# A state-space block ahead of experts and local attention: the scan's drive, the gate, softplus, the convolution's taps, TensorE's start and two small rank tensors rearranged

## The chip, the cores and the metric

The kernel runs on one core of one Trainium2 chip. A core has five engines with queues of their own, each of which runs its instructions in the order in which they were written: TensorE (PE, the matrix array, with weight loads shown as PEld), VectorE (DVE), ScalarE (ACT), GpSimd (POOL) and SyncE (SP, which here only issues DMAs). SBUF is the on-chip memory, PSUM the small one that TensorE writes to. The metric is the device time of one execution in microseconds (us), the median of several; less is better.

## What is computed

A decoder of one block: a state-space layer with a mixture of eight experts behind it, a cross-attention with a relative bias, and six layers of local attention and feed-forward. There are two batches of 512 tokens, 128 features. The change lies in the state-space layer and in the routing of tokens to experts:

```python
def mamba_block(x, in_proj_w, conv_w, conv_b, x_proj_w, dt_proj_w, dt_proj_b, A_log, D_skip, out_proj_w):
    xz = x @ in_proj_w                          # x: (2, 512, 128), xz: (2, 512, 512)
    xi, z = jnp.split(xz, 2, axis=-1)           # 256 channels each
    xc = conv(xi, conv_w)                       # causal, per channel, 4 taps
    xi = jax.nn.silu(xc + conv_b)
    dbc = xi @ x_proj_w                         # 64 + 16 + 16 columns
    delta = jax.nn.softplus(dbc[..., :64] @ dt_proj_w + dt_proj_b)
    Bm, Cm = dbc[..., 64:80], dbc[..., 80:]     # 16 states
    A = -jnp.exp(A_log)
    # for each time step t, channel e and state n:
    #   h = exp(delta * A) * h + (delta * xi) * Bm ;  y = sum over n of h * Cm
    y = y + D_skip * xi
    y = y * jax.nn.silu(z)                      # the gate
    return y @ out_proj_w

def moe_block(x, router_w, Wg, Wu, Wd):         # rms-normed x
    rw = jax.nn.softmax(hs @ router_w)          # 8 experts
    top_w, sel = jax.lax.top_k(rw, 2)
    # out = sum over the two chosen experts of
    #   top_w * ((silu(hs @ Wg[e]) * (hs @ Wu[e])) @ Wd[e])
```

Around both are rms norms and residual additions. The cross-attention and the six layers follow; the change doesn't touch them.

## The kernel before

The program is written out in full, with no loops on the chip. The engines' queues have the order of the text (`manual_schedule`); Python generators are stepped in turn to interleave several streams, so that the place of a `yield` decides what stands behind what in a queue. Waits between engines are put in by the framework where an instruction reads or overwrites what another wrote. Buffers of one tag are handed out in turn, and a new one waits until the oldest has been read for the last time.

**Start.** `norm_in` (L217) norms the tokens of a batch: a square on ScalarE, a sum on VectorE, then six small GpSimd steps for the inverse root (`rstd`, L165), and a product on VectorE. For the first batch GpSimd also multiplies the four taps of the convolution into the input projection (`wk`, L223), so that convolution and projection are one set of matmuls. `turn_in` (L228) transposes the tokens on TensorE against the identity matrix `ident`, sets three columns of zeros ahead of them on GpSimd (L230) and copies them to `nT` on ScalarE (L231). `conv` (L233) has four matmuls for each half of the 256 channels, `gate` (L239) one, `dt_b_c` (L244) two, whose 96 rows are copied to `dbc`; 32 of them, B and C of the 16 states, go to DRAM (`bcd`, L252). A float32 matmul shows as two instructions. PSUM banks come from `bank`: tag m has three, x one, da and y two each.

**Softplus.** `delta` (L254) has a matmul to a PSUM bank `pv` and then, per half of the channels, five ScalarE steps (Relu to `dl`, Abs, twice Exp, Ln) and three VectorE steps (L268 to L270) that join them with a correction for small values. Then `dx` = `dl` * `xi` (L847 for the first batch on VectorE, L876 for the second on GpSimd).

**The scan.** `scan` (L273) goes through the 16 states, each with both halves of the channels over all 512 time steps. Per state n:
- `fetch(n)`: a DMA spreads B's row over all partitions (`b_sb`, three buffers); where GpSimd does the product with C, a second DMA spreads C's row (`c_sb`, two buffers). SP issues them for the first batch, ScalarE's queue for the second.
- `drive(n)`: GpSimd multiplies `dx` with `b_sb` to `db` (three buffers; L300, for state 0 in two halves, L303).
- `decay(n, half)`: ScalarE's Exp to a PSUM bank `da` (L292, two banks).
- The scan proper: a VectorE instruction per half (L325, L328) from `da` and `db` to `hs` (three buffers).
- The product with C in place, on GpSimd (L331) for states 2, 5, 8, 11, 14 of the first batch and all even ones of the second, otherwise on VectorE (L333), with C's row spread by TensorE (`spread_c`, L309).
- `gather(n)`: TensorE adds `hs` to the sum over the states `y` (L313).

The generator yields twice per state, after each half. Ahead of the loop stand `fetch(0)`, `fetch(1)`, `drive(0)` and both `decay` of state 0; in round n come `fetch(n + 2)`, `spread_c(n)` and `drive(n + 1)`, then the scan of the first half of n.

**What runs beside it.** Beside the first batch's scan `other_batch` (L849) brings the second batch up to its own scan: its convolution, then on ScalarE a change of the activation table (L855), the silus of `xi` and of the gate, a change back, then dbc, softplus and `dx`. Beside the second batch's scan run `route(0)`, `sort(0)`, which find the two experts of each token, and the first experts of batch 0 (`experts`, L511: gathers of 128 rows each, issued by GpSimd, L529; transposes, matmuls to `gu_ps`, L546, and `xd`, L567; VectorE's L557 and L558). Tables for the cross-attention (`cross_tables`) are made there too; one of them, `crep`, takes a buffer of the tag hs for a while. `sort` (L378) counts on VectorE how many experts of a token score higher (`rank`, L402), picks ranks 0 and 1 (`sel`, L405), adds up places with matmuls, and gets each token's place `at` (L438), from which L442 on derive tables of rows; most of its tiles are small and lie in SBUF, some in the used PSUM banks. `experts(0)`'s tile `xd` is the one bank of tag x.

Of the kernel before, what the change touches and what calls it, by code (L numbers as in the profile page):

```python
# [15 lines left out]
AF = mybir.ActivationFunctionType  # L16
ALU = mybir.AluOpType
# [4 lines left out]
B, S, D = 2, 512, 128  # L22
NT = B * S
P = 128

DI, NS, KC, DTR, NE, FF = 256, 16, 4, 64, 8, 512
# [15 lines left out]
C_DTB = C_CONVB + 2  # L42
# [24 lines left out]
def decoder_kernel(ctx: ExitStack, tc: tile.TileContext, t: dict, out: bass.AP):  # L67
    nc = tc.nc
    mm, tr = nc.tensor.matmul, nc.tensor.transpose
# [9 lines left out]
    ident = const.tile([P, P], F32, name="ident")  # L79
# [5 lines left out]
    one_c = const.tile([P, 1], F32, name="one_c")  # L85
# [25 lines left out]
    NTB = S // P  # L111

    def bank(name, tag="m"):
        return ps.tile([P, S], F32, tag=tag, name=name, bufs={"m": 3, "x": 1, "da": 2, "y": 2}[tag])
# [17 lines left out]
    w_in = load(sp, [P, 2 * DI], "w_in", t["L0_attn_in_proj_w"])  # L132
    cw = sp.tile([P, KC, DI], F32, tag="hs", name="cw", bufs=3)
# [17 lines left out]
    def col(i, n=P):  # L151
        return cols[0:n, i : i + 1]
# [55 lines left out]
    wk = sp.tile([P, KC, DI], F32, name="wk")  # L208
    nTs = [sp.tile([P, KC - 1 + S], F32, name=f"nT{b}") for b in range(B)]
# [3 lines left out]
    for b in range(B):  # L213
        for name, kept in (("sz", sz), ("xi", xi), ("dl", dl), ("dx", dx)):
            kept.append(full(f"{name}{b}", "A", 8))

    def norm_in(b):  # L217
        xb = xtok[:, 4 * b : 4 * b + 4]
        ss = sq_sum(xb, f"rms1_{b}")
        r = rstd(ss, f"rms1_{b}")  # L220
        if b == 0:

            nc.gpsimd.tensor_mul(wk, cw, w_in[:, 0:DI].unsqueeze(1).to_broadcast([P, KC, DI]))  # L223
        xn = tok(f"xn{b}")
        times(xn, xb, r)
        return xn

    def turn_in(b, xn):  # L228
        pt = turn(xn, f"nT_ps{b}")
        nc.gpsimd.memset(nTs[b][:, 0 : KC - 1], 0.0)  # L230
        nc.scalar.activation(nTs[b][:, KC - 1 :], pt, AF.Identity, scale=col(C_RMS1))  # L231

    def conv(b, hf):  # L233
# [5 lines left out]
    def gate(b, hf):  # L239
        pm = bank(f"gate{b}{hf}")  # L240
        mm(pm, w_in[:, DI + hf * P : DI + (hf + 1) * P], nTs[b][:, KC - 1 :], start=True, stop=True)
        return pm
# [11 lines left out]
    def delta(b, hf):  # L254


        pv = bank(f"dl_ps{b}{hf}")
        mm(pv, w_dt[:, hf * P : (hf + 1) * P], dbcs[b][0:DTR], start=True, stop=True)
        ea, la = (sp.tile([P, S], F32, tag=n, name=n, bufs=2) for n in ("ea", "la"))
        dv = dl[b][:, hf]  # L260
        nc.scalar.activation(dv, pv, AF.Relu, bias=col(C_DTB + hf))

        nc.scalar.activation(pv, pv, AF.Abs, bias=col(C_DTB + hf))
        nc.scalar.activation(ea, pv, AF.Exp, scale=-1.0)
        nc.scalar.activation(pv, pv, AF.Exp, scale=-1.0)
        nc.scalar.activation(la, ea, AF.Ln, bias=one_c)
        yield
        nc.vector.scalar_tensor_tensor(pv, ea, 2.0, pv, ALU.subtract, ALU.mult)  # L268
        nc.vector.scalar_tensor_tensor(pv, pv, -0.5, la, ALU.mult, ALU.max)
        nc.vector.tensor_add(dv, dv, pv)  # L270
        yield

    def scan(b, on_pool):  # L273

        py = [bank(f"y{b}{hf}", "y") for hf in range(2)]
        das, dbs, bbs, cbs, pcs, hss = {}, {}, {}, {}, {}, {}
        queue = nc.scalar if b else nc.sync

        def fetch(n):
            if n < NS:  # L280
                bbs[n] = half(f"b_sb{b}_{n}", "bb", 3)
                queue.dma_start(out=bbs[n], in_=bcds[b][n : n + 1, :].to_broadcast([P, S]))
                if n in on_pool:
                    cbs[n] = half(f"c_sb{b}_{n}", "cb", 2)
                    queue.dma_start(
                        out=cbs[n], in_=bcds[b][NS + n : NS + n + 1, :].to_broadcast([P, S])
                    )

        def decay(n, hf):
            if n < NS:  # L290
                da = das[n, hf] = bank(f"da{b}_{n}{hf}", "da")
                nc.scalar.activation(  # L292
                    da, dl[b][:, hf], AF.Exp, scale=acol[:, hf * NS + n : hf * NS + n + 1]
                )

        def drive(n):
            if n < NS:
                db = dbs[n] = full(f"db{b}_{n}", "db", 3)
                if n:
                    nc.gpsimd.tensor_mul(db, dx[b], bbs[n].unsqueeze(1).to_broadcast([P, 2, S]))  # L300
                else:
                    for hf in range(2):
                        nc.gpsimd.tensor_mul(db[:, hf], dx[b][:, hf], bbs[n])  # L303

        def spread_c(n):
            if n < NS and n not in on_pool:
                pc = pcs[n] = bank(f"c_ps{b}_{n}")
                row = ident[DTR : DTR + 2 * NS, DTR + NS + n : DTR + NS + n + 1]
                mm(pc, row.to_broadcast([2 * NS, P]), dbcs[b][DTR:], start=True, stop=True)  # L309

        def gather(n):
            for hf in range(2):
                mm(py[hf], ident, hss[n][:, hf], start=n == 0, stop=n == NS - 1)  # L313

        fetch(0)
        fetch(1)
        drive(0)
        decay(0, 0)
        decay(0, 1)
        for n in range(NS):  # L320
            fetch(n + 2)
            spread_c(n)
            drive(n + 1)
            hs = hss[n] = full(f"hs{b}_{n}", "hs", 3)
            nc.vector.tensor_tensor_scan(hs[:, 0], das[n, 0], dbs[n][:, 0], 0.0, ALU.mult, ALU.add)  # L325
            decay(n + 1, 0)
            yield
            nc.vector.tensor_tensor_scan(hs[:, 1], das[n, 1], dbs[n][:, 1], 0.0, ALU.mult, ALU.add)  # L328
            decay(n + 1, 1)
            if n in on_pool:  # L330
                nc.gpsimd.tensor_mul(hs, hs, cbs[n].unsqueeze(1).to_broadcast([P, 2, S]))  # L331
            else:
                nc.vector.tensor_mul(hs, hs, pcs[n].unsqueeze(1).to_broadcast([P, 2, S]))  # L333
            if n:
                gather(n - 1)
            yield
        gather(NS - 1)
        for hf in range(2):
            yg = xi[b][:, hf]
            nc.vector.scalar_tensor_tensor(py[hf], yg, col(C_DSKIP + hf), py[hf], ALU.mult, ALU.add)  # L340
            nc.vector.tensor_mul(yg, py[hf], sz[b][:, hf])
# [33 lines left out]
    def small(name, shape, dtype=F32, bufs=1):  # L375
        return ep.tile([P, *shape], dtype, tag=name, name=name, bufs=bufs)

    def sort(b):  # L378
# [19 lines left out]
        nc.vector.tensor_mul(eqv, eqv, lt)  # L398
        nc.vector.tensor_tensor(gt, other, own, ALU.is_gt)
        nc.vector.tensor_add(gt, gt, eq)  # L400
        rank = small("rank", [NTB, NE])
        nc.vector.tensor_reduce(rank, gt, AX.X, ALU.add)  # L402
        sel, two = small("sel", [2, NTB, NE], bufs=2), small("two", [NTB, NE], BF16)
        for j in range(2):
# [28 lines left out]
        nc.vector.tensor_add(  # L433
            place, pos.rearrange("p (n e) -> p n e", e=NE), first.unsqueeze(1).to_broadcast([P, NTB, NE])
        )
        mine, at = small("mine", [2, NTB, NE]), small("at", [2 * NTB])
        nc.vector.tensor_mul(mine, sel, place.unsqueeze(1).to_broadcast([P, 2, NTB, NE]))
        nc.vector.tensor_reduce(at.rearrange("p (j n) -> p j n", j=2), mine, AX.X, ALU.add)  # L438
        yield
# [387 lines left out]
    with tc.manual_schedule(engines={ET.PE, ET.Activation, ET.DVE, ET.Pool, ET.SP}):  # L827
        xn = norm_in(0)
        nc.scalar.activation(acol, cols[:, C_ALOG : C_ALOG + 2 * NS], AF.Exp)
        nc.gpsimd.tensor_scalar(acol, acol, -1.0, None, ALU.mult)  # L830
        turn_in(0, xn)
        xn = norm_in(1)
        p0, p1 = conv(0, 0), conv(0, 1)
        for hf, pm in enumerate((p0, p1)):
            nc.scalar.activation(xi[0][:, hf], pm, AF.Silu, bias=col(C_CONVB + hf))
        p0, p1 = gate(0, 0), gate(0, 1)
        for hf, pm in enumerate((p0, p1)):
            nc.scalar.activation(sz[0][:, hf], pm, AF.Silu)
        table("natural_log_exp_and_others")
        dt_b_c(0)  # L840
        turn_in(1, xn)
# [7 lines left out]
        def other_batch():  # L849

            p0, p1 = conv(1, 0), conv(1, 1)
            yield
            yield
            table("silu_and_others")
            for hf, pm in enumerate((p0, p1)):  # L855
                nc.scalar.activation(xi[1][:, hf], pm, AF.Silu, bias=col(C_CONVB + hf))
            p0, p1 = gate(1, 0), gate(1, 1)
            for hf, pm in enumerate((p0, p1)):
                nc.scalar.activation(sz[1][:, hf], pm, AF.Silu)
            table("natural_log_exp_and_others")  # L860
            yield
            yield
            dt_b_c(1)
            yield
            nc.scalar.copy(hot, stage[:, K_HOT : K_HOT + P])
            nc.scalar.copy(masks, stage[:, K_MASK : K_MASK + 2 * S].rearrange("p (a s) -> p a s", a=2))
            nc.scalar.copy(tri, cst[:, K_TRI - K_HM1 : K_TRI - K_HM1 + P])
            yield
            for hf in range(2):
                g = delta(1, hf)  # L870
                step(g)
                yield
                yield
                step(g)
                yield
            nc.gpsimd.tensor_mul(dx[1], dl[1], xi[1])  # L876
# [34 lines left out]
    NTB = S // P  # L911
# [820 lines left out]
```

## Time and profile before

| what | us |
|---|---|
| runs | 1276.31, 1278.65, 1279.38 |
| median | 1278.65 |
| the profiled execution | 1274.54 |
| its span, first to last instruction | 1272.8 |
| start to the first scan instruction (L325) | 33.2 |
| first batch's scan, to the first sum of y with D (L340) | 33.2 to 99.4 |
| second batch's scan, to the same place | 99.4 to 202.2 |
| second batch's routing and the experts, cross-attention | to 318 |
| six layers | 318 to 1272.8 |

Busy time in three stretches, in us:

| stretch | TensorE | VectorE | ScalarE | GpSimd |
|---|---|---|---|---|
| 0 to 33.2 | 20.0 | 8.9 | 16.1 | 9.2 |
| 33.2 to 99.4 | 56.7 | 53.9 | 35.5 | 51.0 |
| 99.4 to 205.0 | 80.2 | 80.6 | 34.6 | 71.5 |

The page's views: busy time of each engine; the span in 40 slices with a digit for the busy tenths and the granted TensorE clock; DMA queues; the chain that ended last, followed back from the last instruction; the costliest groups of instructions. A line of the timeline has start and duration in us, engine, line of the program, operation, output<-inputs, shape, count, and in brackets how long the engine had been idle and what ended that.

### The profile page before, as it was taken

How to read it: one execution, taken by the hardware profiler on the slowest of the kernel's cores; microseconds unless marked ns; L12 is line 12 of the kernel's file. 1: busy time of each engine (PE TensorE's matmuls, PEld its weight loads, DVE VectorE, ACT ScalarE, POOL GpSimd, SP SyncE). 2: the span in 40 equal slices, each digit the busy share in tenths (PEclk: the TensorE clock that was granted, in tenths of full speed). 3: DMA queues.
4: the chain of work that ended last, by engine and by line, in shares of the span. 5: the costliest groups of instructions: out<-in, count | busy, mean ns of one | idle time of the engine just before them, and what ended most of it. 6: DMA issues, size and time to landing. Idle time of an engine off the chain costs nothing.

```text
span 1272.8 us, 38004 instructions
## 1 busy us (share of the span) xinstructions
PE 1121.3 (88%) x16629; PEld 729.5 (57%) x16629; DVE 868.3 (68%) x1196; ACT 641.4 (50%) x1132; POOL 692.6 (54%) x704
## 2 busy tenths in 40 slices
PE   5987688778568999999999999999999999899987
PEld 2323367766336656666666665656666666555666
DVE  2788585566776776767677766767677666676654
ACT  4643243233334565655557565655556455564543
POOL 2687662453534756646565655647555564555541
PEclk9987799799889999999999999999999999999998
DMA  4224655685102102111211102111211110110100
GB/s 117 77 67 106 195 168 146 203 286 153 53 11 82 40 19 81 53 44 38 71 53 43 45 20 81 53 31 40 81 36 39 45 36 14 36 31 20 36 15 18
DMA packets 51889, 88.52 MB, mean 70 GB/s; under 512 B 7086, under 2 KB 23852, under 8 KB 51724
## 3 DMA queue, kind: packets, MB, share of 16 engines
q1 hardware_dynamic: 46796, 76.78, 19.7%
q10 hardware_dynamic: 3456, 6.29, 1.9%
q0 software_dynamic: 1472, 3.02, 1.1%
q8 instruction: 131, 2.15, 0.7%
q14 instruction: 34, 0.28, 0.1%
HBM read 58.92 MB, written 3.19 MB: 49 GB/s over the span
## 4 chain that ended last, share of the span: by engine, by line
PE 63%; ACT 9%; DVE 7%; issue 4%; POOL 4%; DMA 0%; SPq 0%; POOLq 0%; DVEq 0%; ACTq 0%
PE qk_ps L979 11%; PE t_ps L1161 8%; PE wo_ps L1151 7%; PE v_ps L1012 7%; PE av L1100 5%; PE sim L1064 4%; PE gu_ps L546 3%; ACT pT L1162 3%; PE fo_ps L1253 2%; PE t_ps L1130 2%; PE fg_ps L1230 2%; PE sim L1053 2%; ACT oT L1132 2%; PE xd L567 2%; POOL t L1026 1%
## 5 line engine op out<-in xcount | busy, mean ns | idle before, releaser
L1000 POOL TENSOR_TENSOR t<-t,t 128x1024 f32<-128x1024 f32 x94 | 222.6, 2370 | 157.4 <-DVE t L995 156.6
L979 PE MATMUL qk_ps<-wqkv,z 128*128 128x512 f32 x384 | 186.6, 610 | 1.3 <-ACT sq L984 0.8
L1026 POOL TENSOR_TENSOR t<-t,rn 128x1024 f32<-128x1024 f32 x94 | 177.2, 1906 | 3.7
L991 DVE TENSOR_TENSOR t<-qk_ps,tab 128x1024 f32<-128x1024 f32 x96 | 117.5, 1224 | 78.5 <-PE qk_ps L979 78.5
L1161 PE MATMUL t_ps<-ident,t 128*128 128x128 f32 x768 | 104.1, 279 | 26.0 <-ACT pT L1162 10.8
L1161 PEld LDWEIGHTS t_ps<-ident,t 128*128 128x128 f32 x768 | 87.9, 144 | 64.1 <-issue 36.5
L1023 POOL TENSOR_SCALAR ss<-ss 128x32 f32<-128x32 f32 x47 | 13.4, 286 | 198.3 <-ACT sc L1022 198.3
L1004 DVE TENSOR_REDUCE ss<-sq 128x16 f32<-128x1024 f32 x96 | 116.3, 1212 | 4.0 <-ACT sq L984 0.2
L1162 ACT COPY qT<-t_ps 128x512 f32<-128x512 f32 x96 | 51.9, 588 | 128.4 <-PE t_ps L1161 128.3
L995 DVE TENSOR_TENSOR t<-qk_ps,tab 128x1024 f32<-128x1024 f32 x96 | 116.5, 1214 | 0.0
L1075 DVE TENSOR_REDUCE m<-sim 128x16 f32<-128x1024 f32 x48 | 58.8, 1224 | 70.6 <-PE sim L1064 70.6
L984 ACT ACTIVATE sq<-qk_ps 128x1024 f32<-128x1024 f32 x96 | 97.6, 1036 | 12.9 <-DVE t L995 12.9
L979 PEld LDWEIGHTS qk_ps<-wqkv,z 128*128 128x128 f32 x384 | 69.5, 197 | 52.9 <-issue 49.5
L1012 PE MATMUL v_ps<-wqkv,z 128*128 128x512 f32 x192 | 96.0, 622 | 0.5 <-issue 0.5
L1151 PE MATMUL wo_ps<-oT,wo 128*128 128x256 f32 (+1 forms) x400 | 90.3, 381 | 3.3 <-ACT oT L1132 3.3
L1100 PE MATMUL av<-vb,pT 64*32 64x65 f32 x3072 | 83.0, 228 | 8.1 <-issue 5.2
L1100 PE MATMUL av<-va,pT 64*32 64x65 f32 x3072 | 84.0, 228 | 4.2 <-issue 4.2
L1151 PEld LDWEIGHTS wo_ps<-oT,wo 128*128 128x128 f32 x400 | 74.2, 196 | 19.7 <-ACT oT L1132 6.5
L1162 ACT COPY pT<-t_ps 128x512 f32<-128x512 f32 x96 | 51.6, 589 | 62.1 <-PE t_ps L1161 62.1
L1014 ACT COPY va<-v_ps 128x1024 f32<-128x1024 f32 x48 | 48.6, 1013 | 65.1 <-PE v_ps L1012 65.1
L1064 PEld LDWEIGHTS sim<-kT,qT 64*32 64x32 f32 x6144 | 64.8, 107 | 28.4 <-issue 26.7
L313 PE MATMUL y<-hs,ident 128*128 128x512 f32 x128 | 71.2, 690 | 10.8 <-POOL hs L331 7.3
(351 smaller groups left out, 2298.2 us busy)
## 6 DMA issues: line engine op xcount, KB each, us to landing
w<-in_experts_dram SPq DMA_DIRECT2D x90, 256.0 KB, 4.7
vb<-va SPq DMA_DIRECT2D x48, 390.0 KB, 4.0
wqkv<-in_L_ffn_Wqkv_dram SPq DMA_DIRECT2D x18, 512.0 KB, 7.8
vb<-va SPq DMA_DIRECT2D x36, 130.0 KB, 3.6
b_sb<-bcd SPq DMA_DIRECT2D x16, 256.0 KB, 3.6
b_sb<-bcd ACTq DMA_DIRECT2D x16, 256.0 KB, 3.4
wo<-in_L_ffn_Wo_dram SPq DMA_DIRECT2D x6, 512.0 KB, 4.6
c_sb<-bcd ACTq DMA_DIRECT2D x8, 256.0 KB
```

What stands on the lines that cost most here:

```text
L979: mm(pa[:, hf * S : (hf + 1) * S], self.xb, w[:, w0 : w0 + S], start=True, stop=True)
L991: nc.vector.tensor_mul(t1, pa.rearrange("p (h d) -> p h d", d=DH), tab[:, 2 * qk, ti, :].unsqueeze(1).to_broadcast([P, H, DH]),)
L995: nc.vector.tensor_mul(t2.rearrange("p h (x d) -> p h x d", x=2), swap_halves(pa), tab[:, 2 * qk + 1, ti, :].rearrange("p (x d) -> p x d", ...
L1000: self.calc.tensor_add(t1, t1, t2)
L1004: nc.vector.tensor_reduce(self.ss[:, qk], self.sq[qk], AX.X, ALU.add)
L1012: mm(pv[:, hf * S : (hf + 1) * S], self.xb, w[:, w0 : w0 + S], start=True, stop=True)
L1026: self.calc.tensor_mul(self.rot[qk], self.rot[qk], self.rn[:, qk].unsqueeze(2).to_broadcast([P, H, DH]),)
L1064: mm(ps[32 * j : 32 * j + 32, par, hg, slot, :], qT[64 * r : 64 * r + 64, 2 * hg + c, WIN * w : WIN * (w + 1)], kT[64 * r : 64 * r + 64, 2 ...
L1100: mm(po[hh][32 * at : 32 * at + 32, g, i * DV : (i + 1) * DV], pT[rows, 4 * par + hg, 32 * j : 32 * j + 32], (self.v if par else self.v2)[ ...
L1151: mm(po, wo_l[:, c, :], self.oT[:, c, at : at + w], start=c == 0, stop=c == INNER // P - 1)
L1161: tr(pt[:, n, :], src[:, (4 * g + n) * P : (4 * g + n + 1) * P], ident)
L1162: nc.scalar.copy(dst[:, 4 * g : 4 * g + 4, :], pt)
```

## The change

1. The three zero columns of both `nT` are set right after the tiles are made, and no longer in `turn_in`.
2. `wk` is multiplied in two instructions, one for each half of the channels.
3. 22 matmuls of `ident` with `ident` into the bank of tag x stand on TensorE's queue ahead of the first transposes; nothing reads them.
4. The first batch's gate (two matmuls, two silus) no longer stands behind its convolution, but with the second batch's in `other_batch`.
5. In the first batch's softplus ScalarE has three steps per half (Abs, Exp, Ln), and VectorE makes the relu from `pv` itself; the second Exp is dropped, and both inputs of the first joining step are `ea`. The second batch's is as before.
6. Drives run two states ahead of the scan and fetches three.
7. `rank` and `at` lie in PSUM banks that `sort` has already, and not in SBUF.

```diff
+    for nT in nTs:
+        nc.gpsimd.memset(nT[:, 0 : KC - 1], 0.0)
...
-            nc.gpsimd.tensor_mul(wk, cw, w_in[:, 0:DI].unsqueeze(1).to_broadcast([P, KC, DI]))
+            for hf in range(2):
+                sl = slice(hf * P, (hf + 1) * P)
+                nc.gpsimd.tensor_mul(
+                    wk[:, :, sl], cw[:, :, sl], w_in[:, sl].unsqueeze(1).to_broadcast([P, KC, P])
+                )
...
-        nc.gpsimd.memset(nTs[b][:, 0 : KC - 1], 0.0)
...
-        nc.scalar.activation(dv, pv, AF.Relu, bias=col(C_DTB + hf))
-
-        nc.scalar.activation(pv, pv, AF.Abs, bias=col(C_DTB + hf))
-        nc.scalar.activation(ea, pv, AF.Exp, scale=-1.0)
-        nc.scalar.activation(pv, pv, AF.Exp, scale=-1.0)
-        nc.scalar.activation(la, ea, AF.Ln, bias=one_c)
-        yield
-        nc.vector.scalar_tensor_tensor(pv, ea, 2.0, pv, ALU.subtract, ALU.mult)
-        nc.vector.scalar_tensor_tensor(pv, pv, -0.5, la, ALU.mult, ALU.max)
-        nc.vector.tensor_add(dv, dv, pv)
+        if b:
+
+            nc.scalar.activation(dv, pv, AF.Relu, bias=col(C_DTB + hf))
+            nc.scalar.activation(pv, pv, AF.Abs, bias=col(C_DTB + hf))
+            nc.scalar.activation(ea, pv, AF.Exp, scale=-1.0)
+            nc.scalar.activation(pv, pv, AF.Exp, scale=-1.0)
+            nc.scalar.activation(la, ea, AF.Ln, bias=one_c)
+            qa, eb = pv, pv
+        else:
+            nc.scalar.activation(ea, pv, AF.Abs, bias=col(C_DTB + hf))
+            nc.scalar.activation(ea, ea, AF.Exp, scale=-1.0)
+            nc.scalar.activation(la, ea, AF.Ln, bias=one_c)
+            nc.vector.tensor_scalar(dv, pv, col(C_DTB + hf), 0.0, ALU.add, ALU.max)
+            qa, eb = pv, ea
+        yield
+        nc.vector.scalar_tensor_tensor(qa, ea, 2.0, eb, ALU.subtract, ALU.mult)
+        nc.vector.scalar_tensor_tensor(qa, qa, -0.5, la, ALU.mult, ALU.max)
+        nc.vector.tensor_add(dv, dv, qa)
...
         fetch(0)
         fetch(1)
         drive(0)
+        fetch(2)
+        drive(1)
         decay(0, 0)
         decay(0, 1)
         for n in range(NS):
-            fetch(n + 2)
+            fetch(n + 3)
             spread_c(n)
-            drive(n + 1)
+            drive(n + 2)
...
-        rank = small("rank", [NTB, NE])
+        rank = pr[:, 64 : 64 + NTB * NE].rearrange("p (n e) -> p n e", e=NE)
...
-        mine, at = small("mine", [2, NTB, NE]), small("at", [2 * NTB])
+        mine, at = small("mine", [2, NTB, NE]), pp[:, 192 : 192 + 2 * NTB]
...
+        warm = bank("warm", "x")
+        for _ in range(22):
+            mm(warm[:, 0:P], ident, ident, start=True, stop=True)
         turn_in(0, xn)
...
-        p0, p1 = gate(0, 0), gate(0, 1)
-        for hf, pm in enumerate((p0, p1)):
-            nc.scalar.activation(sz[0][:, hf], pm, AF.Silu)
         table("natural_log_exp_and_others")
...
-            p0, p1 = gate(1, 0), gate(1, 1)
-            for hf, pm in enumerate((p0, p1)):
-                nc.scalar.activation(sz[1][:, hf], pm, AF.Silu)
+            for b in range(B):
+                p0, p1 = gate(b, 0), gate(b, 1)
+                for hf, pm in enumerate((p0, p1)):
+                    nc.scalar.activation(sz[b][:, hf], pm, AF.Silu)
```

## The prediction

> **What bounds the kernel now.** First the page: which engine is busy, and where the chain that ended last runs.
>
> ```profile
> span 1272.8 us, 38004 instructions
> ...
> PE 1121.3 (88%) x16629; PEld 729.5 (57%) x16629; DVE 868.3 (68%) x1196; ACT 641.4 (50%) x1132; POOL 692.6 (54%) x704
> ...
> PE 63%; ACT 9%; DVE 7%; issue 4%; POOL 4%; DMA 0%; SPq 0%; POOLq 0%; DVEq 0%; ACTq 0%
> ```
>
> The shares add to 87%: the chain is followed back to 146.79 us only. But for the second batch's ranks and places (223 to 229 us, no hold there) the diff ends before 205 us, so I read the stretch up to there from timelines, and ask whether what is won there arrives at the end. Behind it neither the program nor its order changes, and the chain runs through TensorE, VectorE and one weight load that waits for the routing; none is tied to a fixed time. So I carry a shift whole.
>
> The first 33 us are one chain:
>
> ```profile
> 11.00 8.66 PE L236 MATMUL conv<-nT,wk 128*128 128x512 f32 x16 [1.40 <-POOL nT L230]
> ...
> 19.50 1.88 PE L241 MATMUL gate<-nT,w_in 128*128 128x512 f32 x4
> ...
> 21.21 1.88 PE L247 MATMUL dbc_ps<-xi,w_x 128*96 128x512 f32 x4
> ...
> 23.13 0.69 DVE L251 COPY dbc<-dbc_ps 96x512 f32<-96x512 f32 x1 [8.33 <-PE dbc_ps L247]
> ...
> 25.05 0.69 ACT L261 ACTIVATE dl<-dl_ps,cols 128x512 f32<-128x512 f32 x1 [0.80 <-PE dl_ps L258]
> ...
> 27.44 0.69 DVE L268 SCALAR_TENSOR_TENSOR dl_ps<-ea,dl_ps 128x512 f32<-128x512 f32 x1 [3.62 <-ACT dl_ps L265]
> ...
> 33.18 1.22 DVE L325 TENSOR_TENSOR_SCAN hs<-da,db 128x512 f32<-128x512 f32 x1
> ```
>
> Convolution, gate, dbc, its copy, softplus, scan, each behind the other. The convolution's weight loads are 0.85 us apart up to 13.72 and 0.43 after: TensorE ran at half speed for its first 3.1 us, though the page's clock row shows 9.
>
> In the first batch's scan VectorE waits here, in the second's there:
>
> ```profile
> 46.30 1.22 DVE L328 TENSOR_TENSOR_SCAN hs<-da,db 128x512 f32<-128x512 f32 x1 [3.58 <-ACT da L292]
> ...
> 52.29 1.22 DVE L325 TENSOR_TENSOR_SCAN hs<-da,db 128x512 f32<-128x512 f32 x1 [1.20 <-POOL db L300]
> ...
> 77.16 1.22 DVE L325 TENSOR_TENSOR_SCAN hs<-da,db 128x512 f32<-128x512 f32 x1 [1.32 <-POOL db L300]
> ...
> 87.99 1.22 DVE L325 TENSOR_TENSOR_SCAN hs<-da,db 128x512 f32<-128x512 f32 x1 [1.36 <-POOL db L300]
> ...
> 112.28 1.22 DVE L325 TENSOR_TENSOR_SCAN hs<-da,db 128x512 f32<-128x512 f32 x1 [1.28 <-POOL db L300]
> ...
> 129.25 2.27 DVE L442 TENSOR_TENSOR past<-at,cst 128x112 f32<-128x112 f32 x1
> ...
> 146.82 1.22 DVE L325 TENSOR_TENSOR_SCAN hs<-da,db 128x512 f32<-128x512 f32 x1 [6.11 <-POOL db L300]
> ...
> 155.49 1.22 DVE L325 TENSOR_TENSOR_SCAN hs<-da,db 128x512 f32<-128x512 f32 x1 [6.33 <-PE y L313]
> ...
> 173.18 2.43 DVE L503 TENSOR_TENSOR sel<-sel,ex 128x64 f32<-128x64 f32 x1
> ```
>
> Five waits for GpSimd's db; one for ScalarE's da; and small VectorE instructions that take over 2 us.
>
> **The front.** The 22 products of ident are 44 instructions on a queue that is idle until 8.48; they can start when ident is made, 1.5 us. A cold 128x128 instruction takes 0.26 (eight of L546 in 2.08 at 149.10), a warm one 0.13 (eight in 1.06 at 159.20). If the clock rises 3.1 us after the start, as at 11.00, they end at 8.8; if after 4.8, as the second convolution's (29.80 to 34.6), at 9.7; if never, 44 x 0.26 = 11.4, at 12.9. I take 9.3, between the two seen; the transposes, ready at 8.48, so begin 0.8 late. Warm they take 0.60 (22.93) and not 1.11; nT's activation 0.69 with 0.1 of handover puts the convolution at 10.7. That covers the memset's removal (0.6 at 11.00: it stood behind wk and acol on GpSimd) and the halving of wk (a 128x512 GpSimd product takes 1.27, so 8.22 to 9.5 for the first half, 10.8 for both): worth nothing by themselves, 0.5 if the products end early. Warm, 16 x 0.43 = 6.9: end at 17.6. Then dbc's second half behind xi's silu (0.75) and two matmuls (0.9): copy at 19.3 and not 23.13. **3.8 gained**; 4.3 with products done at 8.8, 0.2 with 12.9.
>
> [...]
>
> **Softplus.** From the first dl_ps at T (25.05) the first scan now comes at T + 8.13. ScalarE's five steps per half become three, but VectorE gets a fourth: two tensor_scalars (0.69 each, at T and T + 1.0, as the second dl_ps comes about 1.0 later), then from T + 1.7 the same eight instructions as from 27.44 to 33.18 (5.74): T + 7.44. **0.7 gained**. The new L268 has both inputs in SBUF; should GpSimd's half drive (1.27) get in first, it is 0.6 lost.
>
> **The gate moved.** Its four matmul instructions and two silus now stand in the second batch's silu block on ScalarE, between the table loads at 39.06 and 44.28; da for state 2's second half waits behind that block, and VectorE for it (the 3.58). TensorE paces the block: L241 takes 1.99 for four. **1.95 lost**; 1.2 if only the silus count (2 x 0.60), 3.4 at half clock. dbc of the second batch and its softplus queue behind on TensorE and move as much. So of 4.5 won in front 2.55 is left at 46.30.
>
> **Two states ahead.** As it is, GpSimd does the product hs x C of state k (2.35), then the drive of k+2 (2.35), while VectorE has 3.5 us of work. With drive k+2 issued before that product, drive k+3 has 7 us. A buffer comes free in time: db has three, and state n+2 takes n-1's, which VectorE has read. Per three states VectorE needs 10.83 - 1.36 = 9.47 (77.16 to 87.99), GpSimd 6.97 + 2.35 = 9.32: it fits, barely. Removed: 1.32 and 1.36. Not the 1.20 at 52.29: the next instruction, L268 at 53.43, comes 0.16 after ScalarE's Exp, which hangs on TensorE's run since the gates; the wait only moves there. **2.7 gained**; 0 if GpSimd's margin fails, 3.9 with the third.
>
> Second batch: the 1.28 at 112.28 goes, **1.3** (0 to 1.3). At 146.82 the drive of state 8 stands behind four gathers of rows (139.44 to 144.4); a state earlier it is ahead of them, and state 8 runs at 140.7. Then state 9 waits for TensorE's gather of y, behind the first expert; that waits for xT (148.71), whose ScalarE instruction stands behind the da that state 8 releases. Now xs's landing decides (transpose at 145.51, xT at 145.9): **2.8 gained**, of 6.1; 0 if the landing is later. At 173.18 the product of two SBUF tiles ends with GpSimd's drive (173.16 to 175.53). GpSimd, one drive further, then waits for a free db and is idle: VectorE wins 2.2, but gather(10) ends at 177.0 and the next matmul moved from 178.58 to 177.1: **1.4** (0 to 2.2).
>
> What is queued behind: on SP, state 5's two fetches go ahead of the second batch's bcd write (47.70); they wait only for drive 2, done long before. In the second batch fetch(2)'s two DMAs (0.33 and 0.39, at 96.34 and 96.76) go ahead of the da at 95.98, which is not read before 102.23. Fetches of odd states now hold ScalarE's queue until GpSimd's product of the state before has freed a c_sb; drive 2 delays the first product from 104.69 by at most 0.8, the router's norm by 0.35, and lg (115.28) is not read before 118.17.
>
> **Ranks in PSUM.** L405 (1.29 against 0.17) and L442 (2.27 against 0.27 in the second batch) were held until GpSimd's drives ended (121.71, 131.39). But the addition behind L405 and L451 behind L442 also read SBUF twice, like L503: they are held in their place, and only what stands between is won (0.35 and 0.65). With GpSimd's times moved I take **0.5**; -1.0 (a whole drive hit) to 3.1 (no hold).
>
> [...]
>
> Sum: 3.8 + 0.7 - 1.95 + 2.7 + 1.3 + 2.8 + 1.4 + 0.5 = 11.2. The profiled execution took 1274.54 (span 1272.8 and 1.7 around it), so 1263.3; the runs' median is 4.1 higher, 1278.65: I forecast **1267.4**. A measurement here can't tell less than 0.3%, 3.8 us, from no change.
>
> **Rivals.** *Absorbed*: in front only 2.55 is left, and the db waits come back as waits for TensorE (y L313 already holds VectorE 8.8 us in the second batch) or for GpSimd, busy 9.32 of 9.47. For it: the margin of 0.15. Against: TensorE is busy 57 of 66 us, part of that at half clock. Time 1278.65 - 2.55 = 1276.1. *Slower*: the second batch's fetches run on ScalarE. In six odd states (1 to 11) they wait for GpSimd's product, now behind one drive more. If each holds da by 2.35, it costs 14.1, while 1.3, 2.8, 1.4 and 0.5 don't come: 5.25 - 14.1 = -8.9, 1287.5. It decides from 0.9 per state. Against: da waits 34.6 us for VectorE in that stage, so ScalarE has slack. *More*: 1.20 and the holds go as well, and state 9 follows at once: 3.9 for 2.7, 3.1 for 0.5, 6.1 for 2.8 is 18.3, 1260.3. *Not ahead*: if both halves of wk or db's buffers block as before, the drives' 8.2 (2.7, 1.3, 2.8, 1.4) is missing, 3.0 is left, 1275.7; counted with the first.
>
> **Chances.** Forecast 0.66, with its own range 1263 to 1272: front 3.4 (products done at 9.7) to 4.3, the block's loss 3.4 to 1.2, the ranks -1.0 to 3.1, L503 0 to 2.2, which is 4.8 less to 4.7 more than 11.2; more 0.09; absorbed 0.15; slower 0.10. Faster 0.75, same 0.15, slower 0.10. The range reaches from the "more" case to past "absorbed": 1260 to 1277.
>
> **What would show it.** Right: convolution at about 10.7 with weight loads 0.43 apart from the start; copy of dbc near 19.3; first scan near 28.7; da's wait at state 2 longer by about 2; no wait of 1.3 for db in states 7 to 13; state 8 straight after 7; GpSimd waiting for VectorE. Wrong: products past 11 us, ScalarE held at c_sb's fetches, VectorE waiting for y in the first batch, or a second half (from 205 on) that is not as long as before, 1067.8.

## The result and the profile after

The changed kernel took 1297.33 us (median; 1294.66 to 1299.66) and the kernel before, run beside it, 1277.48 (1274.29 to 1279.38): a ratio of 1.016, 95% interval 1.012 to 1.020. The forecast was 1267.4 and at most 1277. The profiled execution took 1299.45, its span 24.9 us more than before.

The page of the changed kernel: span, busy time of each engine with the number of instructions, the chain's shares, then, from the costliest groups, the attention matmuls (busy us, mean ns of one, idle time just before them and what ended it):

```profile
span 1297.7 us, 38084 instructions
...
PE 1131.6 (87%) x16673; PEld 736.4 (57%) x16673; DVE 867.6 (67%) x1198; ACT 639.8 (49%) x1128; POOL 692.9 (53%) x705
...
PE 62%; ACT 8%; DVE 7%; issue 7%; POOL 4%; DMA 2%; SPq 0%; POOLq 0%; DVEq 0%; ACTq 0%
...
L1118 PE MATMUL av<-vb,pT 64*32 64x65 f32 x3072 | 85.9, 228 | 17.1 <-issue 14.2
L1118 PE MATMUL av<-va,pT 64*32 64x65 f32 x3072 | 86.5, 228 | 16.3 <-issue 16.3
...
L1082 PE MATMUL sim<-kT,qT 64*32 64x64 f32 x6144 | 76.0, 231 | 17.6 <-issue 13.7
```

The same three groups in the kernel before:

```profile
L1100 PE MATMUL av<-va,pT 64*32 64x65 f32 x3072 | 84.0, 228 | 4.2 <-issue 4.2
L1100 PE MATMUL av<-vb,pT 64*32 64x65 f32 x3072 | 83.0, 228 | 8.1 <-issue 5.2 <-DVE ln_xc L1212 2.4
L1064 PE MATMUL sim<-kT,qT 64*32 64x64 f32 x6144 | 73.3, 229 | 7.0 <-ACT kT L1162 3.5 <-issue 3.5
```

But for the 22 products on TensorE no engine has more than two instructions more. The chain's "issue" share, time in which an engine waits for nothing that the profile shows, rose from 4 to 7%, and in these three groups of unchanged code idle time put down to "issue" rose from 4.2, 5.2 and 3.5 us (12.9 together) to 44.2: 31.3 us more, which is over the 24.9 to be explained.

Matched instruction by instruction, VectorE's work in the changed kernel lies against the kernel before as follows (minus: earlier; in each case the first instruction from that time of before on):

| from us | 33 | 47 | 100 | 140 | 205 | 410 | 600 | 1040 | end |
|---|---|---|---|---|---|---|---|---|---|
| shift, us | -2.2 | -1.0 | -0.4 | -6.9 | -5.4 | -4.3 | +6.8 | +33.9 | +24.9 |

The -6.9 is that of state 8's first scan instruction, at 146.82 in the kernel before; the last one ahead of it, at 139.48, is at -0.7.

So the part that the change touches did become shorter, by 5.4 us at 205, and the kernel was still 4.3 ahead at 410. What decides is lost behind that, where no line was changed, mostly in steps of 1 to 2.5 us. Granted clock was no cause: 1.00 from 410 to 1040 before, 0.99 after. One step, in a run of attention products on TensorE:

```profile
648.82 0.22 PE L1118 MATMUL av<-vb,pT 64*32 64x65 f32 x1
650.63 0.24 PE L1118 MATMUL av<-va,pT 64*32 64x65 f32 x1 [1.59 <-issue]
```

The same instructions run 0.02 apart ahead of it and behind it; the inputs had been there for the products before. The view of the DMA queues for 647.8 to 649.2 (40 slices of 0.035 us each; a packet is shown in the slice in which it starts; then queue and kind, packets, MB, share of 16 engines) has just one packet:

```profile
DMA  0000009000000000000000000000000000000000
...
DMA packets 1, 0.02 MB, mean 12 GB/s; under 512 B 0, under 2 KB 0, under 8 KB 0
...
q8 instruction: 1, 0.02, 5.4%
```

It starts in the seventh slice, at 648.03 by the trace, and takes 5.4% x 16 x 1.4 us = 1.21 us: it is there at 649.24, and TensorE goes on 1.39 later. The page's line for the whole span is:

```profile
q8 instruction: 131, 2.15, 0.7%
```

2.15 MB in 131 packets is 16.4 KB each. TensorE shows 33690 instructions (16673 matmuls and as many weight loads, and 344 others), and 33690 / 131 is 257. So TensorE's program itself comes by DMA, in blocks, and it stands still where the next block isn't there. The stretch from this halt to the next, 649.5 to 655.2, in the view by windows (busy us and, in brackets, instructions of PE, PEld, DVE, ACT, POOL; then granted clock and DMA), has 127 + 128 of them:

```profile
649.50:655.20 5.70, 3.98 (x127) 2.08 (x128) 2.83 (x5) 2.14 (x5) 1.12 (x3) 1.00 0.02 3
```

In the changed kernel's whole trace 35 pauses of over 1 us, from one TensorE instruction's start to the next one's, end 1.2 to 1.6 us after a packet of this queue, and 32 of the 35 lie at one place: instruction 192 (within three) of a block of 256. These are called halts from here on, and that place the edge. The 32 make 51.7 us; the kernel before has 13 with 19.8; all of them lie behind 410 us.

Not every edge costs. Behind 410 us each kernel has 115 of them, and 91 of the 115 lie in the dense attention groups, in the changed kernel (L1118 and L1082) as in the kernel before (L1100 and L1064). What tells them apart is when the packet comes. At the 32 halts TensorE was at the edge 0.2 to 1.4 us after the start of the packet that it needed, at the other 83 at least 2.0 us after it (before: 0.3 to 1.9 at the halts, 1.9 and more elsewhere). A packet starts about when TensorE begins the block (0.5 us after its first instruction at the halts, 0.6 elsewhere, medians). From that first instruction to the edge TensorE took 1.1 us at the halts and 8.1 at the others (medians): where nothing holds it in this stretch, it is at the edge before the packet. In both traces, at every edge behind 410 us that TensorE reached less than 2.0 us after the packet's start (32 in the changed kernel, 14 in the kernel before) it paused, for 1.1 to 2.5 us (before: 0.5 to 2.1), and no halt stands at another.

The 22 products are 88 instructions of TensorE (44 matmuls, 44 weight loads). They move every later edge by 88 places against the program. By the count above that puts no more edges into dense groups (the first expectation below says that it does); it changes where TensorE's waits fall in a block, and so whether a packet has the time to land. That the place of the edges costs the time is the theory for the tests. Rivals: another edit costs it (**other edit**: ranks in PSUM, the new order, ScalarE held at its fetches); or TensorE's early work itself does, by clock or power (**early work**).

The timeline of the changed kernel's first 155 us, against the steps of the prediction:

```profile
1.47 7.62 PE L850 MATMUL warm<-ident 128*128 128x128 f32 x44 [1.47 <-POOL ident masks.py:199]
...
7.66 1.74 DVE L179 TENSOR_TENSOR xn<-xtok,rms_r 128x512 f32<-128x512 f32 x1 [2.57 <-POOL rms_r L175]
...
9.46 0.66 PE L185 MATMUL nT_ps<-ident,xn 128*128 128x128 f32 x4 [0.38 <-DVE xn L179]
...
20.01 0.69 DVE L257 COPY dbc<-dbc_ps 96x512 f32<-96x512 f32 x1 [4.68 <-PE dbc_ps L253]
...
22.63 0.75 DVE L279 TENSOR_SCALAR dl<-dl_ps,cols 128x512 f32<-128x512 f32 x1 [1.94 <-ACT ea L276]
...
24.68 0.75 DVE L279 TENSOR_SCALAR dl<-dl_ps,cols 128x512 f32<-128x512 f32 x1 [1.30 <-ACT ea L276]
...
31.00 1.22 DVE L341 TENSOR_TENSOR_SCAN hs<-da,db 128x512 f32<-128x512 f32 x1
...
45.30 1.22 DVE L344 TENSOR_TENSOR_SCAN hs<-da,db 128x512 f32<-128x512 f32 x1 [5.58 <-ACT da L306]
...
78.44 1.22 DVE L349 TENSOR_TENSOR hs<-hs,c_ps 128x1024 f32<-128x1024 f32 x1 [1.90 <-PE c_ps L323]
...
99.02 0.76 DVE L356 SCALAR_TENSOR_TENSOR y<-xi,cols,y 128x512 f32<-128x512 f32 x1 [3.65 <-PE y L327]
...
117.97 1.22 DVE L349 TENSOR_TENSOR hs<-hs,c_ps 128x1024 f32<-128x1024 f32 x1 [2.47 <-PE c_ps L323]
...
129.19 0.27 DVE L458 TENSOR_TENSOR past<-place_ps,cst 128x112 f32<-128x112 f32 x1
...
129.88 1.60 DVE L467 TENSOR_TENSOR match<-col,cst 128x120 f32<-128x120 f32 x1
...
139.89 1.22 DVE L341 TENSOR_TENSOR_SCAN hs<-da,db 128x512 f32<-128x512 f32 x1
...
151.60 1.22 DVE L341 TENSOR_TENSOR_SCAN hs<-da,db 128x512 f32<-128x512 f32 x1 [9.38 <-PE y L327]
```

The waits for GpSimd's db are gone, but for one of 0.25 at state 0. In the first batch TensorE's c_ps and y took their place (the wait for y at its end was 1.96 before; now the granted clock is 0.50 from 95.35 to 98.76, and four of the eight last y instructions ran 0.85 us apart, against 0.43 before); in the second batch state 8 comes straight after state 7.

### The profile page after: what moved, and what is told of

Its sections match the earlier page's. It is cut to its first block, busy times and chain, and to the rows that moved or that the text cites. A ratio compares the mean times of both kernels' runs of the same rounds, so it can differ in the third digit from the quotient of the medians.

```text
span 1297.7 us, 38084 instructions
## 1 busy us (share of the span) xinstructions
PE 1131.6 (87%) x16673; PEld 736.4 (57%) x16673; DVE 867.6 (67%) x1198; ACT 639.8 (49%) x1128; POOL 692.9 (53%) x705
## 3 DMA queue, kind: packets, MB, share of 16 engines
q8 instruction: 131, 2.15, 0.7%
## 4 chain that ended last, share of the span: by engine, by line
PE 62%; ACT 8%; DVE 7%; issue 7%; POOL 4%; DMA 2%; SPq 0%; POOLq 0%; DVEq 0%; ACTq 0%
PE qk_ps L997 11%; PE t_ps L1179 7%; PE wo_ps L1169 7%; PE v_ps L1030 7%; PE av L1118 5%; PE sim L1082 5%; PE gu_ps L562 3%; ACT pT L1180 2%; PE t_ps L1148 2%; PE fo_ps L1271 2%; PE fg_ps L1248 2%; PE sim L1071 2%; ACT oT L1150 2%; PE fa_ps L1249 1%; ACT sq L1002 1%
## 5 line engine op out<-in xcount | busy, mean ns | idle before, releaser
L1180 ACT COPY qT<-t_ps 128x512 f32<-128x512 f32 x96 | 51.7, 587 | 124.8 <-PE t_ps L1179 124.7
L1118 PE MATMUL av<-vb,pT 64*32 64x65 f32 x3072 | 85.9, 228 | 17.1 <-issue 14.2
L1118 PE MATMUL av<-va,pT 64*32 64x65 f32 x3072 | 86.5, 228 | 16.3 <-issue 16.3
L1082 PE MATMUL sim<-kT,qT 64*32 64x64 f32 x6144 | 76.0, 231 | 17.6 <-issue 13.7
L1082 PEld LDWEIGHTS sim<-kT,qT 64*32 64x32 f32 x6144 | 65.9, 107 | 41.0 <-issue 40.1
L1118 PEld LDWEIGHTS av<-vb,pT 64*32 64x32 f32 x3072 | 67.9, 106 | 34.6 <-issue 22.6
```

The lines of the kernel that those rows point to most:

```text
L1082: mm(ps[32 * j : 32 * j + 32, par, hg, slot, :], qT[64 * r : 64 * r + 64, 2 * hg + c, WIN * w : WIN * (w + 1)], kT[64 * r : 64 * r + 64, 2 ...
L1118: mm(po[hh][32 * at : 32 * at + 32, g, i * DV : (i + 1) * DV], pT[rows, 4 * par + hg, 32 * j : 32 * j + 32], (self.v if par else self.v2)[ ...
```

## The experiments

The runs below were made on three chips (12, 0 and 10 in the record), on which the kernel before takes 1285 to 1289 us; ratios are against its runs beside them. Shifts are against the one profile of the kernel before, that of the result. In the profiles of these runs every kernel, changed or not, loses some 8 to 12 us between 205 and 300 us against it, so shifts are read up to 205 only; where that loss comes from was not tried.

### Where the late loss comes from

Four kernels separate the instruction count from everything else. **a1_no_products** is the changed kernel without item 3:

```diff
-        warm = bank("warm", "x")
-        for _ in range(22):
-            mm(warm[:, 0:P], ident, ident, start=True, stop=True)
```

> Everything of the change but the 22 products, so TensorE's stream has the instruction count of before. Theory (88 more TensorE instructions put the 256-instruction block edges into the dense attention runs): the front's 3.1 us are lost again, the late loss goes: 1273 to 1279 us, issue gaps before L1100/L1118-type av products back to some 4 us per group (9 stalls of 1 to 2.5 us, not 31). Rival (another edit, such as the ranks in PSUM or the new order, costs the late 36 us): about 1297 + 3 = 1300. Rival recorded (ScalarE held at c_sb fetches): about 1300.

1278.03 us, ratio 0.994 (0.991 to 0.997); 10 halts. **b1_with_products** is the kernel before with these three lines alone:

> The kernel before and the 22 products alone. Theory (block edges): the front gains up to 3 us, the layers from 410 us on lose about 36: 1300 to 1311 us, about 30 stalls. Rival (another edit costs it): 1274 to 1277.

1313.48 us, ratio 1.023 (1.018 to 1.028); 29 halts. **a2_64_small** fills the block up:

```diff
-        for _ in range(22):
-            mm(warm[:, 0:P], ident, ident, start=True, stop=True)
+        for _ in range(64):
+            mm(warm[0:32, 0:44], ident[:, 0:32], ident[:, 0:44], start=True, stop=True)
```

> The changed kernel with 64 products of 32x44 in place of the 22 of 128x128: as many moving columns, but 256 TensorE instructions in place of 88, a whole block, so the edges of all later blocks lie as in the kernel before. Theory (block edges): 1270 to 1276 us, some 9 stalls. Rival (early work on TensorE, its clock or power costs the late part): 1294 to 1300, as the changed kernel.

1275.32 us, ratio 0.993 (0.990 to 0.996); 12 halts, although the kernel has more TensorE instructions than any before it. **b2_22_small** puts 88 short instructions into the kernel before:

```diff
+        warm = bank("warm", "x")
+        for _ in range(22):
+            mm(warm[0:32, 0:16], ident[:, 0:32], ident[:, 0:16], start=True, stop=True)
         turn_in(0, xn)
```

> The kernel before with 22 products of 32x16 ahead of the first transposes, where TensorE is idle: 88 instructions more, but little work. Theory (block edges): front unchanged, layers lose about 36: 1303 to 1314 us. Rival (TensorE's early work, clock or power): about 1278, as before.

1310.09 us, ratio 1.022 (1.016 to 1.028); 30 halts. Up to 140 us its work lies within 0.2 us of the kernel before. The absolute times of the expectations were made from the result's runs. As they stand, a1, a2 and b2 lie in the ranges of the block edges and b1 2.5 us above its own; with the some 7 us added by which the kernel before is slower here, b1 and b2 lie in them, a1 and a2 some 2 us below. Either way each of the four is 19 us or more from the time of its rivals. Both rivals fall: "other edit", because b1 and b2 have no other edit and lose what the changed kernel loses, and a1 has all the others and doesn't; "early work", because b2 has 2.5 us of it (the products' span in its profile) and loses all, while a2 has 7.3 us and loses nothing. The groups of matmuls by line show the same idle time. a2, the changed kernel's code with 256 instructions more:

```profile
L1118 PE MATMUL av<-va,pT 64*32 64x65 f32 x3072 | 83.5, 228 | 6.0 <-issue 6.0
L1118 PE MATMUL av<-vb,pT 64*32 64x65 f32 x3072 | 83.1, 228 | 2.9 <-DVE ln_xc L1230 2.4
L1082 PE MATMUL sim<-kT,qT 64*32 64x64 f32 x6144 | 73.7, 229 | 9.5 <-issue 5.0 <-ACT kT L1180 4.5
```

b2, the code of before with 88 more (its lines are three further down):

```profile
L1103 PE MATMUL av<-va,pT 64*32 64x65 f32 x3072 | 86.8, 228 | 14.7 <-issue 14.7
L1103 PE MATMUL av<-vb,pT 64*32 64x65 f32 x3072 | 86.0, 227 | 17.8 <-issue 15.0 <-DVE ln_xc L1215 2.4
L1067 PE MATMUL sim<-kT,qT 64*32 64x64 f32 x6144 | 75.9, 232 | 14.2 <-issue 9.8 <-ACT kT L1165 4.4
```

Idle time put down to "issue" is 11.0 us in the first and 39.5 in the second; 12.9 before, 44.2 after.

### Other places of the edges

a4 (the diff below) and a5 have other numbers of small products in the same place (32 of 32x88, 48 of 32x58); a7 and a8 (72 of 32x39, 56 of 32x50) have the old softplus as well, like a3 below. Each is one profiled execution.

```diff
-        for _ in range(64):
-            mm(warm[0:32, 0:44], ident[:, 0:32], ident[:, 0:44], start=True, stop=True)
+        for _ in range(32):
+            mm(warm[0:32, 0:88], ident[:, 0:32], ident[:, 0:88], start=True, stop=True)
```

> The changed kernel with 32 products of 32x88 in place of the 22: 128 TensorE instructions, half a block from the edges of before. Only the block edges are moved. If the number of stalls depends on the edges alone, it differs from 13 (edges of before) and from 30 to 32 (88 instructions on); between them the layers would lie between 0 and 36 us behind before. If the 88 were something else than a place (a count, more work), 128 would be worse than 88.

> The changed kernel with 48 products of 32x58: 192 TensorE instructions, three quarters of a block. As for 32: a different number of stalls than 13 and 30 to 32 if the place of the edges decides. If the count decides, worse than 88 and 128.

> The run with the old softplus, and 72 products of 32x39 in place of 64 of 32x44: 32 TensorE instructions more, block edges an eighth of a block on. If the cost follows the place of the edges, a number of stalls between or beside 12 (edges of before) and 32 (88 on): 10 to 25, and a time 0 to 20 us above 1273. If it followed the amount of early work, the time would be that of 64.

> The same with 56 products of 32x50: 32 TensorE instructions fewer, edges an eighth of a block back. Between 12 stalls (edges of before) and 15 (192 instructions): 10 to 17, 1270 to 1280 us. If it shows fewer than 10 stalls, it is the better place.

| TensorE instructions added, modulo 256 | halts | us in them | time, us |
|---|---|---|---|
| 0 (a2; a3) | 12; 12 | 18.5; 17.3 | 1275.3; 1273.0 (medians) |
| 32 (a7) | 22 | 32.9 | 1286.0 |
| 88 (b1; b2, on the kernel before) | 29; 30 | 47.4; 46.0 | 1313.5; 1310.1 (medians) |
| 128 (a4) | 18 | 28.8 | 1290.4 |
| 192 (a5) | 15 | 26.1 | 1288.3 |
| 224 (a8; a9) | 9; 13 | 14.7; 19.8 | 1267.7; 1274.3 (median) |

It is a place and not an amount: 128 and 192 cost less than 88. a8 came out better than expected on both counts (9 halts for 10 to 17, 1267.7 us for 1270 to 1280). The table gives no rule that would tell a good place ahead of time, and the count of halts itself varies between runs of one kernel (9 and 13 at 224).

### Drives two states ahead, alone

**b3_two_ahead** is the kernel before with item 6 alone; TensorE's count stays.

```diff
         drive(0)
+        fetch(2)
+        drive(1)
...
-            fetch(n + 2)
+            fetch(n + 3)
...
-            drive(n + 1)
+            drive(n + 2)
```

> The kernel before with the drives two states ahead alone (no TensorE instruction more). The recorded sum gives it 2.7 + 1.3 + 2.8 + 1.4 = 8.2 us by 205 us. Read from the changed kernel, where the shift of VectorE's work goes from -1.0 at 47 us to -5.4 at 173 us: 4.4 us, most of it in the second batch, where the first batch gives next to nothing since it then waits for TensorE's c_ps and y. If the recorded terms hold: first batch 2.7 or more at 100 us; if TensorE took the wait over: 1 or less at 100 us.

1279.2 us, ratio 0.9963 (0.9941 to 0.9985). Shift +0.5 us at 100, -5.3 at state 8 (146.82 of before), -4.6 at 205: nothing in the first batch, 5.1 in the second, and the total (0.4% of 1285 is 4.8) keeps it. VectorE waits now for TensorE in the first batch:

```profile
79.68 1.22 DVE L335 TENSOR_TENSOR hs<-hs,c_ps 128x1024 f32<-128x1024 f32 x1 [1.92 <-PE c_ps L309]
...
87.34 1.22 DVE L335 TENSOR_TENSOR hs<-hs,c_ps 128x1024 f32<-128x1024 f32 x1 [1.52 <-PE c_ps L309]
```

These two waits (3.44) stand where those for db (1.32 and 1.36) stood.

### The softplus of before

**a3_old_softplus** is a2 with `delta` as before for both batches (item 5 undone).

```diff
-        if b:
...
-        else:
-            nc.scalar.activation(ea, pv, AF.Abs, bias=col(C_DTB + hf))
-            nc.scalar.activation(ea, ea, AF.Exp, scale=-1.0)
-            nc.scalar.activation(la, ea, AF.Ln, bias=one_c)
-            nc.vector.tensor_scalar(dv, pv, col(C_DTB + hf), 0.0, ALU.add, ALU.max)
-            qa, eb = pv, ea
```

> The changed kernel with the 64 small products and the softplus of before. Recorded: the new softplus gains 0.7, so the first scan comes 0.7 later than with it. Theory from the changed kernel's trace (VectorE's tensor_scalar waits for ScalarE's Abs on the same PSUM bank, 1.94 and 1.30 us, so the first scan stood at 9.09 and not 7.44 behind the first dl_ps): the first scan comes about 1 us earlier without the new softplus, 8.1 behind. The total moves by less than a measurement can tell.

1273.04 us, ratio 0.991 (0.988 to 0.995). From its trace, dl_ps's first reader and the first scan:

```profile
21.75 0.69 ACT L267 ACTIVATE dl<-dl_ps,cols 128x512 f32<-128x512 f32 x1 [0.78 <-PE dl_ps L264]
...
29.88 1.22 DVE L333 TENSOR_TENSOR_SCAN hs<-da,db 128x512 f32<-128x512 f32 x1
```

8.13 us from the one to the other, as in the kernel before, against 9.09 in the changed one (21.91 to 31.00) and in a2. The new softplus is 0.96 slower.

### The first batch's gate in its old place

**a6_old_gate** is a3 with item 4 undone.

```diff
+        p0, p1 = gate(0, 0), gate(0, 1)
+        for hf, pm in enumerate((p0, p1)):
+            nc.scalar.activation(sz[0][:, hf], pm, AF.Silu)
         table("natural_log_exp_and_others")
...
-            for b in range(B):
-                p0, p1 = gate(b, 0), gate(b, 1)
+            p0, p1 = gate(1, 0), gate(1, 1)
```

> The run with the 64 small products and the old softplus, and the first batch's gate back in its old place. Recorded: the move takes 1.9 us of TensorE out of the front and costs 1.95 at the wait for da. Theory: dbc's copy about 1.9 later than there (19.85), da's wait at state 2 about 2 shorter (3.6), so no difference from 47 us on: within 0.5 us at 47 and within 1.5 at 205 us. Rival (the move pays, since the matmuls then run warm or lie beside other work): 1 to 2 us later at 205 us with the gate in its old place.

1273.24 us, ratio 0.989 (0.983 to 0.996): not to be told from a3. dbc's copy came at 20.59 with its convolution begun 0.81 earlier than in a3, so the gate in front costs 1.55. But da's wait at state 2 was 5.21 and not the 3.6 expected, because here TensorE ran the second batch's four gate instructions at half speed (granted clock 0.50 from 39.67 to 43.08):

```profile
39.47 3.62 PE L247 MATMUL gate<-nT,w_in 128*128 128x512 f32 x4 [1.31 <-DVE hs L341]
```

They take as long as all eight in a3 (3.70). So at 47 us a6 is 1.2 behind a3, and at 205 us 2.7, more than either the theory (within 1.5) or its rival (1 to 2) expected; since the half speed falls in one of the two runs only, the price of the move by itself stays open. b1 lost its front in the same way: 1.8 us ahead at 33 us, its four gate instructions took 3.65 at 40.06 instead of 1.99, and at 47 us it was level.

### A version that beats both

> The one look's kernel with 56 products of 32x50 and the old softplus, now timed. Theory: faster than both kernels, since it keeps what the change wins ahead of 205 us (some 8 us) and has fewer stalls (9) than the kernel before (13): 12 to 20 us under before on the same chip, a ratio of 0.985 to 0.991. Rival (the look was a lucky one): 0.991 to 0.994, like the runs whose edges lie as before.

The kernel of a8 timed: 1274.25 us, ratio 0.990 (0.986 to 0.994), 13 halts in its profile and not 9. It is 1.0% faster than the kernel before, and by the ratios than the changed kernel (1.016); the intervals don't separate it from a2, a3 and a6, so the better place of the edges isn't shown to be better than that of before.

## Why the prediction was wrong

**The step that failed** is "behind it neither the program nor its order changes ... none is tied to a fixed time. So I carry a shift whole." The order of TensorE's program doesn't change, but its place in the blocks does, and that is tied to a count of instructions. The prediction put this at nothing; it cost 31.9 us of halts (51.7 against 19.8) and turned a gain into a loss. The recorded line of what would show it wrong, a second half that is not as long as before, is where it showed: 29.2 us longer from 410 to the end (38.2 lost up to 1040, 9.0 won back behind it, where the kernel before has 12.1 us of halts and the changed one 7.6; the rest of that was not traced). The prediction counted the 22 products as 44 instructions and priced them only by the time that they take in an idle queue; the "issue" idle time of L1100 and L1064, 12.9 us in groups of code that waits for nothing, stood in the groups of before and wasn't asked about. With the edges back in their place the carrying fits: a1, b3 and a2 were 5.3, 4.6 and 8.5 us ahead at 205 us in their profiles, and 0.6, 0.4 and 0.7% (8, 5 and 9 us) ahead in their times, which were measured against the kernel before on the same chip.

None of the recorded rivals was the cause. *Slower* (ScalarE held at c_sb's fetches) gave the right sign for a wrong reason: at 205 us the changed kernel was ahead, and a1, with the same fetches, was faster than before.

**Front**, forecast 3.8, measured 3.1 (dbc's copy at 20.01). Products ended at 9.09 (9.3 forecast), but by two errors that cancel: they started 0.21 us apart for the first 5.1 us and 0.11 after, where the sum had 0.26 and 0.13 and a rise after 3.1 to 4.8 us. The convolution ran warm (weight loads 0.43 apart). Lost was the product at 7.66, which took 1.74 and not 0.69 beside GpSimd's first half of wk; in a2 it took 0.69 and the copy stood at 19.28: 3.8.

**Softplus**, forecast 0.7 gained, 1.0 lost. I let the second tensor_scalar start at T + 1.0. It stands on VectorE ahead of the first half's joins, and waits for ScalarE's Abs of the second half, which is behind the first half's Exp and Ln: T + 2.77 (24.68 against 21.91). The first scan came at T + 9.09 and not T + 7.44.

**Gate block**, forecast 1.95 lost; the wait went from 3.58 to 5.58, so 2.00. But a6 and b1 show that the term depends on the speed of TensorE at that place (four gate instructions took 3.62 and 3.65 there, 1.99 in the kernel before), which moves when the work ahead of it moves.

**First batch**, forecast 2.7, measured nothing (0.6 lost between 47 and 100 us; 0.5 behind at 100 in b3): the "absorbed" rival held here. **Second batch**, forecast 1.3 + 2.8 + 1.4, with 0.5 for the ranks 6.0: measured 5.0 between 100 and 205 us, 5.1 in b3 without the ranks. Its parts are mis-sized one by one: the 1.3 at 112 came and was used up by a wait for c_ps at 117.97; state 8 came 6.9 earlier; state 9, at 151.60, kept 3.9 of it; L503's hold (2.43 us) went, which won 2.2, and 1.3 of that was left at 205 (1.4 forecast).

**Ranks**: `past` went from 2.27 to 0.27, and the instruction with two SBUF inputs behind it, `match`, took 1.60 in its place (0.27 before), to 131.48, where GpSimd's drives ended at 131.34. In the time at 205 us the ranks don't show: 5.0 won in the second batch with them, 5.1 without.

At 205 us 5.4 of 11.2 had come. In a2 it was 8.5; 0.7 of the difference is the front, the rest was not traced.

## What to carry to other kernels

Adding or removing TensorE instructions anywhere ahead of long runs of short matmuls is an edit of those runs too (here 88 more gave 32 halts for 13, 256 more gave 12): look for "issue" pauses at equal counts of 256 instructions before believing that code far behind is unchanged, and test a change once more with the count filled up to a whole block. A wait taken from one engine is won only if the next engine is ahead: here the db waits of the first batch turned into waits for TensorE (1.32 and 1.36 into 1.92 and 1.52 in b3). And compare stretch by stretch; the total alone would have condemned six edits for the place of a seventh.

## What the runs showed of the hardware

- TensorE's program of 33690 instructions is fetched in 131 packets of 16.4 KB, each 1.1 us long on average. At a halt TensorE resumes 1.2 to 1.6 us after the packet's end; the pauses counted took 1.0 (the least that was counted) to 2.5 us. Behind 410 us no halt stood at an edge that TensorE reached 2.0 us or more after the packet's start, in the profiles of both kernels (101 such edges before, 83 after).
- The half-speed spans of TensorE do not keep their place. The second batch's convolution, 16 equal instructions, begins at a granted clock of 0.50, which lasts 4.8 us from its start in the kernel before (29.80 to 34.58), 4.8 in a3 (26.41 to 31.18), 5.7 in a6 (27.17 to 32.84) and 3.5 in a7 (25.35 to 28.89). In the profiles of both kernels each stretch between two changes of the granted clock is a whole multiple of 3.41 us, as the 0.50 from 95.35 to 98.76 in the changed kernel.
